# Neighbours' sums of six of ten node tiles by gathered rows instead of an adjacency product, in a graph network of two attention layers and a relational layer

## The chip, the cores and the metric

The kernel runs on one core of one Trainium2 chip. The metric is device time in microseconds (us) of one execution; the time before is the median of three runs. Five engines work side by side, each with an instruction queue of its own that runs in order: PE (TensorE, matrix products and transposes), DVE (VectorE), ACT (ScalarE), POOL (GpSimd, here mostly the issuer of indirect DMAs, which gather or scatter rows by an index), and SP (SyncE, issues plain DMAs). PEld is PE's weight load. DMA engines, 16 of them, move data for all queues.

## The reference, cut to what matters

1250 nodes of 768 features, 20000 edges (src, dst), each with one of 34 types.

```
x = x + GATv2(relu(layernorm(x)))          # two attention layers, 8 heads and 1 head
h = relu(layernorm(x))
mean[r, n] = mean over edges of type r into n of h[src]
h1  = sum over r of mean[r] @ W_rel[r] + h @ W_root + b_rgcn
xw  = h1 @ W_gcn
deg = (number of edges into a node) + 1;  dinv = rsqrt(deg)
out[n] = sum over edges into n of xw[src] * dinv[src] * dinv[n] + xw[n] * dinv[n]^2 + b_gcn
x + out
```

Everything is float32. The last layer is linear, so the kernel sums the scaled rows of h1 over the neighbours first and multiplies by W_gcn afterwards.

## The kernel before, in words

**Nodes by degree.** The front part sorts the nodes by falling degree into NT = 10 tiles of P = 128 (NP = 1280 places). Tile k has room for `CAPS[k]` edges per node: (33, 22, 20, 18, 17, 16, 15, 14, 13, 11), 179 slots in all. `f.srci[p, k, s]` is the source node of slot s of the node at place p of tile k, `f.pad` marks empty slots, `f.perm` the node of a place (`f.permg` the same, kept below 1250), `f.degf` the degree by place, `f.degn` the degree by node.

**Two attention stages.** For each slot a row of 768 features (and a few more numbers) per node is gathered on POOL into one of 24 buffers (`fs`, L1179 by the helper at L1125), DVE works out the logits (L1189 to L1195) and PE adds up the weighted rows. Between them POOL scatters one small record per slot (`f.rec`: source and own node) to its place in a list in DRAM (`pair_d`), which groups edges by type (`list_edges`, L1362). `finish2`, once per tile at the end of the second stage, writes x1 with the last bias, scatters h (`h2_d`) and the root term h @ W_root + b_rgcn into `h1_d` (L1451 to L1454).

**The relation stage.** For each type r there are PT = 4 tiles of pairs (and PX = 3 spare tiles); `lists` holds the pair list. `first_half` gathers h rows (`g`, with further rows added on DVE, L1549 to L1555) and transposes them; `second_half` multiplies by W_rel[r], copies PSUM to `y` on ACT (for the first two tiles scaled by `rcnt`, one over the number of edges of the pair, L1572; else L1574) and scatters `y` into `h1_d` with an adding DMA (L1575). Beside it, DVE builds a row of the adjacency matrix per place, one instruction per slot (`adjacency`, L1489, float16, 1250 columns), and when a tile's slots are done PE transposes the rows and ACT writes them into `adj`, scaled by dinv of the source (`adjacency_columns`, L1495 and L1497).

**The tail.** Once the last sum is in `h1_d`, it is loaded as ten tiles `h3` of 125 partitions (L1603, on SP's and ACT's queues in turn), `neighbours` multiplies them with `adj` for 512, 512 and 256 places (L1626; results to `gT` by ACT and DVE, L1629 and L1630), and `last(k)` multiplies one tile of places by W_gcn (L1638), scales by dinv of the place and adds x1 on DVE (L1641), and scatters to the output on POOL.

**What sets the order.** The code states the order of dependences only; a planner puts each engine's instructions in the order in which it expects them to become ready, and among ready ones in the order of the code. A tile with `bufs=n` is a ring of n buffers: the next user waits until the buffer's readers are done. `issue_after` holds an instruction behind a given one on its engine.

Of the kernel before, what the change touches and what calls it, by code (L numbers as in the profile page):

```python
# [27 lines left out]
PT = 4  # L28
PX = 3
# [596 lines left out]
def fast_front(ctx, tc, f, x, src, dst, edge_type, W1s, b1s, W1d, b1d, attn1, W_rel):  # L626
# [43 lines left out]
    f.srci = keepp.tile([P, NT, S0], I32, name="srci")  # L670
# [386 lines left out]
def halves(t, n, f):  # L1057
    return t[:n, :f.D].rearrange("p (a b) -> p a b", a=2)
# [45 lines left out]
def fast_rest(ctx, tc, f, x, src, dst, edge_type, W1s, b1s, W1d, b1d, attn1, ln1_w, ln1_b,  # L1104
# [10 lines left out]
    h1_d = dram.tile([NP + (PT + 1) * P, D], F32, name="r_h1_d")  # L1115
    pair_d = dram.tile([P * f.COLS, 2], I32, name="r_pair_d")
# [32 lines left out]
    def attention(H, table, negated, attn, first, loads, finish, rate, rest):  # L1149
# [25 lines left out]
        def front(c, i):  # L1175

            t, s = c.t, c.first + i
            fs = pool.tile([P, RW], F32, name="fs", tag="fs", bufs=ring)
            row = gather(fs[:, :W], table[:, :], f.srci[:, t.k, s:s + 1])  # L1179
            fs = fs[:, :W].rearrange("p (h e) -> p h e", h=H)  # L1180
            if s >= CHUNK or t.k:
                list_edges(row, rate)
            if t.k == NT - 1 and s == t.S - 1:
                list_edges(row, rest)
            if t.lg is None:
                lg = pool.tile([P, S0 * f.H], F32, name="lg", tag="lg", bufs=2)
# [143 lines left out]
    def prepare_lists():  # L1330
# [3 lines left out]
        with tc.tile_pool(name="r_fill", bufs=1, side="right") as fp:  # L1334
# [3 lines left out]
            fill = fp.tile([P, COLS, 2], I32, name="fill")  # L1338
# [16 lines left out]
        f.rec = rp.tile([P, NT, S0, 2], I32, name="rec")  # L1355
        nc.vector.tensor_copy(f.rec[:, :, :, 0], f.srci)
# [67 lines left out]
    with ExitStack() as two:  # L1424
        ap2 = two.enter_context(tc.tile_pool(name="r_att2", bufs=1, side="right"))

        def loads2():
            for name, a in (("lnw", lno_w), ("lnb", lno_b), ("bias_r", b_rgcn), ("bias_g", b_gcn)):
                late[name] = load_row(ap2, a, name)
            late["wroot"] = load_w(ap2, W_root, "wroot", "wroot")  # L1430

        def finish2(k, o):
            lnw, lnb, bias_r, bias_g = late["lnw"], late["lnb"], late["bias_r"], late["bias_g"]
# [31 lines left out]
    dinv = rq.tile([P, NT], F32, name="dinv")  # L1465
    nc.scalar.activation(dinv, f.degf, AF.Sqrt, bias=f.ones_col, scale=1.0)
    nc.vector.reciprocal(dinv, dinv)
    dinvn = rq.tile([P, NT], F32, name="dinvn")
    nc.scalar.activation(dinvn[:NQ], f.degn[:NQ], AF.Sqrt, bias=f.ones_col[:NQ], scale=1.0)
    nc.vector.reciprocal(dinvn[:NQ], dinvn[:NQ])  # L1470
# [9 lines left out]
    adj = rq.tile([P, NT, NP], F32, name="adj")  # L1480
# [10 lines left out]
    def adjacency_columns(k):  # L1491
# [4 lines left out]
        for j in range(NT):  # L1496
            nc.scalar.activation(adj[:NQ, j, k * P:(k + 1) * P], pt[:NQ, j, :], AF.Copy, scale=dinvn[:NQ, j:j + 1])  # L1497

    slots_left = [(k, s) for k in range(NT) for s in range(CAPS[k])]


    with ExitStack() as three:
# [3 lines left out]
        lists = gp.tile([P, COLS, 2], I32, name="lists")  # L1506
# [13 lines left out]
        nc.vector.reciprocal(rcnt, rcnt)  # L1520

# [5 lines left out]
        def first_half(i):  # L1527
# [13 lines left out]
            j.node = lists[:, col, 1:2]  # L1541
# [25 lines left out]
        def second_half(j, w):  # L1567
# [29 lines left out]
    with ExitStack() as four:  # L1597
# [17 lines left out]
        def neighbours(lo, hi):  # L1615

            if lo == 0:
                pss = [sums_psum() for _ in range(KC // 2)]
                order = [(j, c) for j in range(NT) for c in range(KC)]
            else:  # L1620
                pss = [None] * (KC // 2)
                order = [(j, 2 * g + c) for g in range(KC // 2) for j in range(NT) for c in range(2)]
            for j, c in order:
                if pss[c // 2] is None:
                    pss[c // 2] = sums_psum()
# [5 lines left out]

        def last(k):
            xt = gp.tile([P, D], F32, name="x1r", tag="x1r", bufs=3)
# [7 lines left out]
            nc.vector.scalar_tensor_tensor(halves(o, P, f), ps[:, :, :HW], dinv[:, k:k + 1], halves(xt, P, f),  # L1641
# [56 lines left out]
```

## Time and profile before

| what | value |
|---|---|
| median of three runs (lowest, highest) | 2852.77 us (2851.39, 2857.41) |
| profiled execution, and its span from the first to the last instruction | 2850.16 us, 2848.3 us |
| mean granted TensorE clock | 0.924 |
| PE, DVE, ACT, POOL busy | 84%, 57%, 30%, 52% of the span |
| first attention stage's gathers begin | 177 us |
| second attention stage's gathers begin | 941.5 us |
| relation stage's gathers begin | 1425.0 us |
| last `y` is scattered | 2615.1 us |
| first and last matmul of the tail | 2628.7 us, end 2837.3 us |

Times in the profile are from one execution and counted from its first instruction; a difference between two kernels' medians is compared with the sum made on it. A group line of the profile has line, engine, operation, out<-in, number of instructions, then busy time, mean duration of one in ns, and the engine's idle time just before them with what ended it. A line of a helper (L1125 gather, L1129 scatter, L1094 dense product, L1082 transposes) serves several stages, which the tile names tell apart. In a timeline line the numbers are start, duration, engine, line, and in brackets the engine's idle time before it and what ended it.

### The profile page before, as it was taken

To read this page: it belongs to the slowest core of one execution; us is meant where nothing else is said; L and a number is where in the kernel's file an instruction comes from. 1 tells how busy PE (TensorE), PEld (TensorE's weight loads), DVE (VectorE), ACT (ScalarE), POOL (GpSimd) and SP (SyncE) were. 2 spreads that over 40 slices of the span, in tenths; PEclk is the share of its full clock that TensorE was granted. 3 is DMA by queue.
4 is the path that set the end of the run, shared out by engine and by line. 5 is a ranking of instruction groups with operands and counts; after the bars stand their busy time and mean duration, and the time that the engine had idled before them with its cause. 6 is when DMAs were issued, how large, how long until landed. Compare 5 with 4: busy or idle time off the path is not lost. (4 is left out here: it accounts for less than half of the span.)

```text
span 2848.3 us, 24209 instructions
## 1 busy us (share of the span) xinstructions
PE 2391.8 (84%) x7859; PEld 1393.1 (49%) x7859; DVE 1621.7 (57%) x2382; ACT 846.5 (30%) x2320; POOL 1482.4 (52%) x1049
## 2 busy tenths in 40 slices
PE   5912574779998477888789999999999999997998
PEld 3411232445544244445456666666666666664455
DVE  5459988999986699999474433343343333210000
ACT  2000792778674022333211222222212212221000
POOL 2440787687786586777275555454455554421000
PEclk9955897999999688899889999999999999999999
DMA  5150643444540675676277777777777777665211
GB/s 199 28 188 31 199 137 94 124 133 119 146 146 28 224 233 181 200 222 204 100 228 201 188 187 196 195 201 180 181 201 182 183 198 185 182 163 130 82 45 50
DMA packets 130127, 448.22 MB, mean 157 GB/s; under 512 B 25014, under 2 KB 26061, under 8 KB 129991
## 3 DMA queue, kind: packets, MB, share of 16 engines
q0 software_dynamic: 77792, 305.26, 41.0%
q1 hardware_dynamic: 47257, 133.96, 13.3%
q10 hardware_dynamic: 4942, 7.36, 0.8%
q8 instruction: 65, 1.06, 0.1%
q14 instruction: 71, 0.58, 0.1%
HBM read 357.48 MB, written 89.11 MB: 157 GB/s over the span
## 5 line engine op out<-in xcount | busy, mean ns | idle before, releaser
L1094 PE MATMUL ps<-wrel,mT 128*128 128x384 f32 x3336 | 1099.5, 486 | 0.7 <-DMA wrel<-in_L_gnn_W_rel_dram 0.7
L1094 PEld LDWEIGHTS ps<-wrel,mT 128*128 128x128 f32 x3336 | 623.4, 190 | 406.8 <-DMA wrel<-in_L_gnn_W_rel_dram 1.0
L1125 POOL DMA_INDIRECT g<-r_h_d,lists x241 | 367.5, 1525 | 472.6 <-DVE g L1549 300.7
L1249 PE MATMUL ag<-fs,identf 128*128 128x384 f32 x716 | 285.6, 531 | 175.2 <-ACT fs L1247 163.1
L1247 ACT ACTIVATE fs<-fs,lg 128x96 f32<-128x96 f32 x1376 | 370.2, 362 | 1.7 <-issue 1.4
L1189 DVE TENSOR_TENSOR z<-fs,nfd 128x776 f32<-128x776 f32 (+1 forms) x358 | 344.5, 977 | 42.8 <-DMA fs<-f_fs_d,srci 25.2
L1549 DVE TENSOR_TENSOR g<-g,g 128x768 f32<-128x768 f32 x68 | 64.6, 950 | 525.8 <-DMA g<-r_h_d,lists 426.6
L1239 PE MATMUL ag<-fs,dg 128*128 128x384 f32 x716 | 251.6, 513 | 84.7 <-ACT dg L1237 84.7
L1129 POOL DMA_INDIRECT r_pair_d<-rec,place x179 | 242.3, 1354 | 126.7 <-DMA r_pair_d<-fill 72.4
L1575 POOL DMA_INDIRECT r_h_d<-y,lists x139 | 229.4, 1650 | 131.3 <-ACT y L1574 64.8
L1249 PEld LDWEIGHTS ag<-fs,identf 128*128 128x128 f32 x716 | 131.9, 200 | 316.3 <-ACT fs L1247 250.0
L1125 POOL DMA_INDIRECT fs<-f_fs_d,srci x179 | 238.5, 1332 | 90.9 <-issue 45.3
L1125 POOL DMA_INDIRECT fs<-r_fs_d,srci x179 | 240.2, 1342 | 84.9 <-PE ag L1239 38.3
L1489 DVE SCALAR_TENSOR_TENSOR arow<-node,from_f,arow 128x1250 f16<-128x1250 f16 x179 | 270.8, 1514 | 3.7
L1239 PEld LDWEIGHTS ag<-fs,dg 128*128 128x128 f32 x716 | 142.8, 202 | 188.4 <-ACT dg L1237 90.3
L1574 ACT COPY y<-ps 128x768 f32<-128x768 f32 x71 | 56.8, 800 | 481.3 <-PE ps L1094 481.3
L1572 ACT ACTIVATE y<-ps,rcnt 128x768 f32<-128x768 f32 x68 | 61.3, 901 | 444.8 <-PE ps L1094 444.8
L1191 DVE SCALAR_TENSOR_TENSOR z<-z,attn_e 128x769 f32<-128x769 f32 x179 | 178.5, 1017 | 0.0
L1194 DVE TENSOR_TENSOR z<-z,attn_e 128x776 f32<-128x776 f32 x179 | 168.4, 954 | 0.1
L1195 DVE TENSOR_REDUCE lg<-z 128x8 f32<-128x776 f32 x179 | 168.1, 950 | 0.1
L1630 DVE COPY gT<-hb 128x512 f32<-128x512 f32 (+1 forms) x9 | 5.4, 602 | 249.8 <-ACT gT L1629 249.8
L1626 PE MATMUL hb<-adj,h 125*128 125x512 f32 (+1 forms) x360 | 131.4, 528 | 14.7 <-DMA h<-r_h_d 14.7
(271 smaller groups left out, 2288.5 us busy)
## 6 DMA issues: line engine op xcount, KB each, us to landing
wrel<-in_L_gnn_W_rel_dram SPq DMA_DIRECT2D x37, 2304.0 KB
g<-r_h_d,lists POOLq DMA_INDIRECT x241
r_nfd_d<-fd SPq DMA_DIRECT2D x10, 384.0 KB
nfd<-r_nfd_d SPq DMA_DIRECT2D x10, 384.0 KB
r_x_d<-xb SPq DMA_DIRECT2D x10, 384.0 KB
x1r<-r_x_d SPq DMA_DIRECT2D x10, 384.0 KB
f_fs_d<-o_s SPq DMA_DIRECT2D x9, 388.0 KB
x<-in_x_dram SPq DMA_DIRECT2D x9, 384.0 KB
```

What stands on the lines that cost most here:

```text
L1094: last = nc.tensor.matmul(ps[:n, half, :f.HW], hT[:, k, j * P:j * P + n], w[:, k, cols], start=(k == 0), stop=(k == f.KC - 1 and not bias))
L1125: return nc.gpsimd.indirect_dma_start(out=to, out_offset=None, in_=table, in_offset=bass.IndirectOffsetOnAxis(ap=idx, axis=0))
L1129: s = nc.gpsimd.indirect_dma_start(out=table, out_offset=bass.IndirectOffsetOnAxis(ap=idx, axis=0), in_=rows, in_offset=None, **kw)
L1189: nc.vector.tensor_tensor(z, fs, t.nfd, op=ALU.max)
L1191: nc.vector.scalar_tensor_tensor(z[:, 0, :], z[:, 0, :], 1.0, attn_e[:, 0, :], op0=ALU.mult, op1=ALU.mult, accum_out=t.lg[:, s, :])
L1194: nc.vector.tensor_mul(z, z, attn_e)
L1195: nc.vector.tensor_reduce(t.lg[:, s, :], z, axis=AX.X, op=ALU.add)
L1239: nc.tensor.matmul(c.ps[:, half, :HW], dg, fs[:, 0, half * HW:(half + 1) * HW], start=begin, stop=end)
L1247: nc.scalar.activation(fs[:, h, :HD], fs[:, h, :HD], AF.Copy, scale=t.lg[:, s, h:h + 1])
L1249: nc.tensor.matmul(c.ps[:, half, :HW].rearrange("p (h d) -> p h d", d=HD), f.identf, fs[:, half * H // 2:(half + 1) * H // 2, :HD], start= ...
L1489: nc.vector.scalar_tensor_tensor(a, node16, from_f[:, k, s:s + 1], a, op0=ALU.is_equal, op1=ALU.add)
L1575: s = nc.gpsimd.indirect_dma_start(out=h1_d[:, :], out_offset=bass.IndirectOffsetOnAxis(ap=j.node, axis=0), in_=y, in_offset=None, compute ...
```

## The change: what it does

Four of the ten node tiles (k = 0 to 3, DT = 4, the highest degrees) keep the adjacency product: `adj` has 512 columns, `adjacency` and `adjacency_columns` run for 93 of 179 slots. For the other six, in the order 9 to 4, the new `by_rows(k)` gathers each node's own row of `h1_d` into an accumulator (`acc`, two buffers) and then one row per slot (`nb`, twelve buffers), which DVE adds; empty slots read a row of zeros at the end of `h1_d`. PE transposes the sum and ACT writes it to `gT`. `last(0)` to `last(3)` stand between them in the code, `last(9)` to `last(4)` behind them.

For the sum of rows to be right, the rows of `h1_d` must already be scaled by dinv of their node. So the pair records get a third number, dinv of the own node, from which every `y` is scaled on ACT (times one over the count for the first two tiles); the root term is scaled by dinv on ACT as it leaves PSUM, with its bias now added by PE as a product of a row of ones; and `adj` is no longer scaled. `f.srci` becomes the first column of `f.rec`.

```diff
-    f.srci = keepp.tile([P, NT, S0], I32, name="srci")
+    f.rec = keepp.tile([P, NT, S0, 3], I32, name="rec")
+    f.srci = f.rec[:, :, :, 0]
...
-            row = gather(fs[:, :W], table[:, :], f.srci[:, t.k, s:s + 1])
+            row = gather(fs[:, :W], table[:, :], f.rec[:, t.k, s, 0:1])
...
+            nc.sync.dma_start(h1_d[ZERO:, :], zero[:1])
...
-        nc.vector.tensor_copy(f.rec[:, :, :, 0], f.srci)
+        f.dinv = rp.tile([P, NT], F32, name="dinv")
+        nc.scalar.activation(f.dinv, f.degf, AF.Sqrt, bias=f.ones_col, scale=1.0)
+        nc.vector.reciprocal(f.dinv, f.dinv)
+        nc.vector.tensor_copy(f.rec[:, :, :, 2].bitcast(F32), f.dinv[:, :, None].to_broadcast([P, NT, S0]))
...
-            ps = dense(nc, ps_t, f, hT, late["wroot"], 0, P, tag="mm2")
+            ps, _ = dense(nc, ps_t, f, hT, late["wroot"], 0, P, tag="mm2", bias=(late["ones"], late["bias_r"]))
-            nc.vector.tensor_add(halves(o, P, f), ps[:, :, :HW], halves(bias_r, P, f))
+            nc.scalar.activation(halves(o, P, f), ps[:, :, :HW], AF.Copy, scale=f.dinv[:, k:k + 1])
...
-    adj = rq.tile([P, NT, NP], F32, name="adj")
+    adj = rq.tile([P, NT, DT * P], F32, name="adj")
+    srcz = rq.tile([P, NT, S0], I32, name="srcz")
+    nc.vector.scalar_tensor_tensor(srcz, f.pad, float(ZERO), f.srci, op0=ALU.mult, op1=ALU.max)
...
-            nc.scalar.activation(adj[:NQ, j, k * P:(k + 1) * P], pt[:NQ, j, :], AF.Copy, scale=dinvn[:NQ, j:j + 1])
-    slots_left = [(k, s) for k in range(NT) for s in range(CAPS[k])]
+            nc.scalar.copy(adj[:NQ, j, k * P:(k + 1) * P], pt[:NQ, j, :])
+    slots_left = [(k, s) for k in range(DT) for s in range(CAPS[k])]
...
+        norms = lists[:, :, 2].bitcast(F32)
+        nc.vector.tensor_mul(rcnt, rcnt, norms[:, :R * PC].rearrange("p (r c) -> p r c", c=PC)[:, :, :2])
...
-            if j.t < 2:
-                nc.scalar.activation(halves(y, P, f), ps[:, :, :HW], AF.Copy, scale=rcnt[:, j.r, j.t:j.t + 1])
-            else:
-                nc.scalar.copy(halves(y, P, f), ps[:, :, :HW])
+            nc.scalar.activation(halves(y, P, f), ps[:, :, :HW], AF.Copy, scale=j.scale)
...
+        def by_rows(k):
+            acc = gp.tile([P, D], F32, name="acc", tag="acc", bufs=2)
+            gather(acc, h1_d[:, :], f.permg[:, k:k + 1])
+            for i in range(CAPS[k]):
+                g = gp.tile([P, D], F32, name="nb", tag="nb", bufs=12)
+                gather(g, h1_d[:, :], srcz[:, k, i:i + 1])
+                nc.vector.tensor_add(acc, acc, g)
+            to_columns(nc, ps_t, f, gT, k, acc, P, both=True)
...
-            xt = gp.tile([P, D], F32, name="x1r", tag="x1r", bufs=3)
+            xt = gp.tile([P, D], F32, name="x1r", tag="x1r", bufs=2)
...
-        neighbours(0, 512)
-        neighbours(512, 1024)
-        for k in range(4):
-            last(k)
-        neighbours(1024, NP)
-        for k in range(4, NT):
-            last(k)
+        neighbours(0, DT * P)
+        for k in range(NT - 1, DT - 1, -1):
+            by_rows(k)
+            if NT - 1 - k < DT:
+                last(NT - 1 - k)
+        for k in range(NT - 1, DT - 1, -1):
+            last(k)
```

The row of the list that is filled ahead of the scatters (`fill`) also gets a third column, of zeros, and the list is 12 bytes per record where it was 8.

More of the change, by code (lines that the diff above doesn't have):

```diff
@@ L28 @@
 PT = 4
+DT = 4
 PX = 3
@@ L1114, in fast_rest @@
     h2_d = dram.tile([NP + P, D], F32, name="r_h2_d")
-    h1_d = dram.tile([NP + (PT + 1) * P, D], F32, name="r_h1_d")
-    pair_d = dram.tile([P * f.COLS, 2], I32, name="r_pair_d")
+    ZERO = NP + (PT + 1) * P
+    h1_d = dram.tile([ZERO + 1, D], F32, name="r_h1_d")
+    pair_d = dram.tile([P * f.COLS, 3], I32, name="r_pair_d")
     x1_d = dram.tile([NP, D], F32, name="r_x1_d")
@@ L1337, in prepare_lists @@
                            allow_small_or_imprecise_dtypes=True)
-            fill = fp.tile([P, COLS, 2], I32, name="fill")
+            fill = fp.tile([P, COLS, 3], I32, name="fill")
+            nc.vector.memset(fill[:, :, 2], 0)
             ones_c = fp.tile([P, COLS], F32, name="ones_c")
@@ L1352, in prepare_lists @@
                 nc.sync.dma_start(h1_d[NP + t * P:NP + (t + 1) * P, :], zero)
+            nc.sync.dma_start(h1_d[ZERO:, :], zero[:1])
         f.place = rp.tile([P, NT, S0], I32, name="place")
         nc.sync.dma_start(f.place, f.place_d.rearrange("p (k s) -> p k s", k=NT))
-        f.rec = rp.tile([P, NT, S0, 2], I32, name="rec")
-        nc.vector.tensor_copy(f.rec[:, :, :, 0], f.srci)
+        f.dinv = rp.tile([P, NT], F32, name="dinv")
+        nc.scalar.activation(f.dinv, f.degf, AF.Sqrt, bias=f.ones_col, scale=1.0)
+        nc.vector.reciprocal(f.dinv, f.dinv)
+        nc.vector.tensor_copy(f.rec[:, :, :, 2].bitcast(F32), f.dinv[:, :, None].to_broadcast([P, NT, S0]))
         nc.vector.tensor_copy(f.rec[:, :, :, 1], f.perm[:, :, None].to_broadcast([P, NT, S0]))
@@ L1427, in loads2 @@
         def loads2():
-            for name, a in (("lnw", lno_w), ("lnb", lno_b), ("bias_r", b_rgcn), ("bias_g", b_gcn)):
+            for name, a in (("lnw", lno_w), ("lnb", lno_b), ("bias_g", b_gcn)):
                 late[name] = load_row(ap2, a, name)
+            late["ones"] = ap2.tile([1, P], F32, name="ones_r")
+            nc.vector.memset(late["ones"], 1.0)
+            late["bias_r"] = ap2.tile([1, D], F32, name="bias_r")
+            nc.scalar.dma_start(late["bias_r"], bass.AP(tensor=b_rgcn.tensor, offset=b_rgcn.offset, ap=[[0, 1], [1, D]]))
             late["wroot"] = load_w(ap2, W_root, "wroot", "wroot")
         def finish2(k, o):
-            lnw, lnb, bias_r, bias_g = late["lnw"], late["lnb"], late["bias_r"], late["bias_g"]
+            lnw, lnb, bias_g = late["lnw"], late["lnb"], late["bias_g"]
             sc, sh = norm_scale(nc, small, f, o, P)
@@ L1464, in fast_rest @@
     rq = ctx.enter_context(tc.tile_pool(name="r_late", bufs=1))
[L1465 to L1470, printed above, removed]
     ident16 = rq.tile([P, P], F16, name="ident16")
@@ L1505, in fast_rest @@
         assert not edges
-        lists = gp.tile([P, COLS, 2], I32, name="lists")
+        lists = gp.tile([P, COLS, 3], I32, name="lists")
         nc.sync.dma_start(lists, pair_d.rearrange("(p c) f -> p c f", p=P))
@@ L1540, in first_half @@
                 col = r * PC + t
-            j.node = lists[:, col, 1:2]
+            j.node, j.scale = lists[:, col, 1:2], norms[:, col:col + 1]
+            if t < 2:
+                j.scale = rcnt[:, r, t:t + 1]
             g = gp.tile([P, D], F32, name="g", tag="g", bufs=7)
@@ L1615, in neighbours @@
         def neighbours(lo, hi):
[L1617 to L1625, printed above, removed]
+            pss = [sums_psum() for _ in range(KC // 2)]
+            for j, c in [(j, c) for j in range(NT) for c in range(KC)]:
                 nc.tensor.matmul(pss[c // 2][:, c % 2, :hi - lo], hs[j][:, c * P:(c + 1) * P], adj[:NQ, j, lo:hi],
@@ L1640, in last @@
             o = gp.tile([P, D], F32, name="o4", tag="o4", bufs=3)
-            nc.vector.scalar_tensor_tensor(halves(o, P, f), ps[:, :, :HW], dinv[:, k:k + 1], halves(xt, P, f),
+            nc.vector.scalar_tensor_tensor(halves(o, P, f), ps[:, :, :HW], f.dinv[:, k:k + 1], halves(xt, P, f),
                                            op0=ALU.mult, op1=ALU.add)
             scatter(out[:, :], o, f.perm[:, k:k + 1], "out", bounds_check=N - 1, oob_is_err=False)
-        neighbours(0, 512)
-        neighbours(512, 1024)
-        for k in range(4):
-            last(k)
-        neighbours(1024, NP)
-        for k in range(4, NT):
+        neighbours(0, DT * P)
[4 more added lines that the diff above has]
+        for k in range(NT - 1, DT - 1, -1):
             last(k)
```

## The prediction

> **What bounds the kernel now.** I read the page's slices first, for which engine is full where.
>
> ```profile
> PE   5912574779998477888789999999999999997998
> DVE  5459988999986699999474433343343333210000
> POOL 2440787687786586777275555454455554421000
> ```
>
> A slice is 71 us. DVE fills the attention slices (5 to 19), PE everything after slice 21. In the last three DVE is at 0 and POOL at 1, then 0: the tail is TensorE alone. The chain of waits, in order of time, says the same to the hundredth:
>
> ```profile
> 2615.09 5.49 DMA r_h_d<-y,lists
> ...
> 2628.65 105.36 PE hb L1626 x240
> 2734.01 30.96 PE hb L1638 x96
> 2764.97 25.90 PE hb L1626 x120
> 2790.88 46.46 PE hb L1638 x144
> ```
>
> The last h1 sum lands at 2620.6; the h rows are loaded; then PE runs without a gap to 2837.3: 131.3 us of adjacency product (L1626) and 77.4 of W_gcn product (L1638), the latter 7.74 per node tile. From PE's last matmul to the end of the span are 11.0 us. Next, busy time by window, for attention 2, the relation stage and the h loads (columns: window, its length, PE, PEld, DVE, ACT, POOL busy, clock, DMA share, GB/s):
>
> ```profile
> 1000.00:1370.00 370.00, 295.59 (x864) 170.92 (x863) 362.47 (x697) 111.93 (x235) 264.57 (x188) 0.89 0.65 201
> 1440.00:2614.00 1174.00, 1173.24 (x4261) 723.49 (x4260) 423.36 (x353) 247.76 (x514) 583.46 (x369) 1.00 0.72 186
> 2622.00:2634.00 12.00, 5.35 (x8) 2.38 (x9) 0.00 (x0) 0.00 (x0) 0.00 (x0) 0.54 0.32 124
> ```
>
> DVE binds attention 2 (98% busy), PE the relations (99.9%). While the h rows load, the DMA share is only 0.32 at 124 GB/s, so about a third of the DMA engines carry them.
>
> **The sum is made on the profiled execution**, 2850.16 us (span 2848.3 and 1.9 around it); the median of the three runs, 2852.77, lies 2.6 above it, and I add that at the end.
>
> **Part 1, attention 2: -7 us.** Ten PSUM evacuations of `root` leave DVE (L1453, 952 ns each, about 0.88 net since neighbouring instructions overlap by 0.07) for ACT, 30% busy in this window. Eight fall where DVE is full: 8 x 0.88 = 7.0. PE gets four bias instructions per tile (1.3 us at the 0.33 us pace of the dense ones) and has 74 idle us here. ACT now waits for the product where DVE did (L1453 waited 16.4 us in all), and ACT's diagonal scalings for PE queue behind it; the ring of 24 gathered rows covers a wait of a few us, without it this costs up to those 16. At the stage's end DVE no longer holds `x1` for a root, -2.6; the bias matmuls, ACT's turn and a pair list half as long again to load give back about 2. I count -0.5, between -2.5 and +2.
>
> **Part 2, relations: -4 us.** Six of ten tiles' transposes go (L1495, 7.4 us for ten: 4.4, or 3.5 by the 0.58 after which PE's next began). 86 adjacency instructions of 1.51 us leave DVE, which is 36% busy here: nothing. y is scaled on ACT always, 0.90 against 0.80 us, once on the path: +0.1.
>
> **Part 3, front: +0.5 us.** One memset of 241 columns (0.25), a reciprocal (0.14), and a copy for a copy of the same 330 elements on a full DVE. The square root and reciprocal move there from 1413. SP issues one more small write, some 0.5 us ahead of weights not needed for many us. Pair scatters carry 12 bytes for 8 in the same 128 rows: nothing. The gathers now read the tile whose other columns DVE fills. In the trace the copy of `perm` into it runs at 115.5, far ahead of its place in the code, and the first gather at 177; so I see no wait.
>
> **Part 4, the tail.** PE's work falls from 208.7 to 52.7 (half of 105.36) + 77.4 + 6 x 0.82 of transposes = 135 us. But 86 neighbour rows and 6 own rows have to be gathered, 92 POOL instructions, and added, 86 x 0.95 = 82 us on an idle DVE. What does a gather cost beside such adds? Nearest is the opening of attention 2: rows of the same 3 KB, a DVE that is 77% busy with instructions of two SBUF inputs (28.1 of the 36.5 us from 941.5), other loads beside it.
>
> ```profile
> 941.51 0.99 POOL L1125 DMA_INDIRECT fs<-r_fs_d,srci  x1 [2.99 <-DMA r_fs_d<-fs,f_perm]
> ...
> 976.92 1.29 POOL L1125 DMA_INDIRECT fs<-r_fs_d,srci  x1 [0.47 <-DMA wroot<-in_L_gnn_W_root_dram]
> ```
>
> 23 steps in 35.41 us: 1.54 each, and the row is usable 3.1 us after its issue ends (the first VectorE instruction on it starts at 945.62). Bounds: 1.25, the even step from 177 to 207, most of it with DVE idle; and 2.32, the mean step of the seven from 1438.64 to 1454.90, beside back-to-back 1.5 us instructions of L1489. I take 1.54. So POOL is the new bound: 92 x 1.54 + 10 x 1.3 of output scatters = 155 us.
>
> It cannot run through, for the change adds a wait. There are two accumulators: tile 7's own row waits until tile 9's transposes have read the first, and on PE these stand behind the whole product of tiles 0 to 3. Behind that gather POOL's queue holds tiles 6 to 4 and all outputs, and DVE's the adds of tile 7, which alone free the ring of twelve. Up to then POOL can do 12 + 14 gathers for tiles 9 and 8 and 12 into the ring for tile 7: 38. They collide with the h rows. How queues share busy engines is shown where all three were full (share of 16 engines):
>
> ```profile
> q0 software_dynamic: 301, 1.50, 47.2%
> q1 hardware_dynamic: 303, 0.93, 29.1%
> q10 hardware_dynamic: 301, 0.83, 26.3%
> ```
>
> Gathers (q0) take 47 of 102, so the h rows keep 54% of their 130 GB/s, 70: 3.84 MB need 55 us and the last lands near 2677; at 130 it would be 2651. PE has two slices of 5.14 left then, so the product ends near 2687, not 2682.5. A gather needs a third of its 393 KB from those same engines: 123 KB at 61 GB/s, 2.0 us each until 2677, 1.54 after: 34 landed by 2687.
>
> Then: 2687 + 1 (tile 9's transposes) + 58 x 1.54 = 89.3 + four outputs between, 5.2, gives 2782.5. On the path behind the last gather: landing 3.1, add 0.95, transposes 1.5 and W_gcn product 7.74 + 4 (the granted clock was 0.54 in the first 4 us after PE's last idle stretch, and PE will have idled), two copies 1.0: 18.3, so 2800.8, and 11.0 to the end: **2811.8, -36.5 against 2848.3**. The products of the other tiles fit into PE's pauses.
>
> [...]
>
> **Sum:** 2850.16 - 36.5 - 7 - 0.5 - 4 + 0.1 + 0.5 = 2802.8; with 2.6 for the median, **2805**.
>
> **The rivals.**
> *Cheap gathers* (10%): 1.25 and an uncontended load. T9 at 2683.5, 54 left: 67.5 + 5.2 + 18.3 + 11 = 2785.5 for the tail, 2779 in all. For it: the 1.25 rows; against: DVE will be busy.
> *The planned order stalls at the product's end* (12%): if POOL's order has the first output, or DVE's the copies of the product, before tile 8's rows are added, only 25 gathers precede 2688. At 1.64 each (1342 ns is the mean of attention 2's gathers, and 0.30 between them) 67 of them, 5.2 and 29.3 end the tail at 2832, -16; with gains of only 5 before it 2832 in all. For it: POOL and DVE are in order; against: in the relation stage's opening the first scatter of y came at 1456.07 behind 18 gathers, six us after y was ready, so the order leans to gathers.
> *Dear gathers, the slower side* (7%): at 2.32, 28 are done by 2687 and 64 remain: 2688 + 148.5 + 5.2 + 29.3 = 2871, +22.7, or 2864 in all. It decides from 2.2 us per gather (30 done, 62 x 2.2 = 136). For it: the rows at 1438; against: no 1.5 us VectorE instructions run in the tail.
> *Queues in code order* (5%): each output then waits for its tile's product and all later gathers behind it: 2695 after tile 9, then 14, 15, 16 gathers at 1.54 each with 16.8 for landing, add, transposes, product and output (2815), 35 gathers (2869), 7 and six products in a row (2922), 11: 2933, or 2926 in all. Against it stand the 18 gathers, where the code has five.
> *No net change* (2%): gathers near 2.2, PE's saving spent by POOL to the microsecond.
>
> **How the numbers follow.** The forecast has 64%; its own range is 2787 to 2822 (gathers at 1.35 to 1.75, product's end 2682 to 2690). The cheap and the stalled case take it to 2776 to 2834, which leaves out the two slow cases and a little beyond each end. A difference of 0.2%, 5.7 us, is about what measurement tells from none. Faster 0.64 + 0.10 + 0.12, less 0.01 for a tail worse than its bounds: 0.85; same 0.03, the last rival and that 0.01; slower 0.07 + 0.05 = 0.12.
>
> **What would show it.** Gathers `nb` at a mean step of 1.5 to 1.6; POOL the chain's main engine from 2677 to the last gather; a pause of POOL before tile 7's `acc`; h rows landing over some 55 us; L1626 at 120 instructions with gaps; attention 2 ending 7 us earlier. Wrong if the step exceeds 2.2, or if POOL sits before an `out` scatter for more than 10 us.

## The result, and the profile after

The changed kernel takes 2831.33 us (median of seven runs, 2824.57 to 2843.05) against 2852.77 before: ratio 0.9926, 95% interval 0.9904 to 0.9947. That is 21 us less, not 48. The profiled execution took 2831.33 as well; its span is 2829.2. Cut at the same five events in both traces:

| stretch (us) | before | changed | difference | predicted |
|---|---|---|---|---|
| start to the first gather of attention 2 | 941.5 | 941.6 | +0.1 | +0.5 |
| to the last weighted sum of attention 2 | 444.8 | 448.6 | +3.8 | -7 |
| to the first relation product | 54.1 | 54.2 | +0.1 | -0.5 |
| to the last relation product | 1173.6 | 1170.7 | -2.9 | -3.9 |
| to the end of the span | 234.3 | 214.0 | -20.3 | -36.5 |

So the front and the relations went as forecast, attention 2 went the other way, and the tail gained a little over half. The page's slices, the three rows that were shown of before:

```profile
PE   5912574788898377888969999999999999999676
DVE  5459988999987699899552223222222222200254
POOL 2440687687777576688264554445444454431465
```

In the last three slices PE is no longer full and DVE and POOL are no longer empty: the work did move. The question is what it waits for there. The windows of the tail (window, length, PE, PEld, DVE, ACT, POOL busy, clock, DMA share, GB/s):

```profile
2622.00:2634.00 12.00, 0.00 (x0) 0.00 (x0) 0.00 (x0) 0.00 (x0) 8.61 (x9) 0.50 0.81 240
2634.00:2690.00 56.00, 48.87 (x104) 20.70 (x105) 21.08 (x22) 0.00 (x0) 26.76 (x23) 0.93 0.83 260
2690.00:2722.00 32.00, 27.14 (x82) 15.12 (x81) 13.45 (x15) 3.38 (x7) 15.84 (x14) 0.95 0.66 215
2722.00:2790.00 68.00, 48.16 (x144) 28.16 (x143) 41.03 (x44) 1.82 (x4) 53.21 (x49) 0.87 0.91 312
```

POOL issues 23 gathers in the 56 us of the second line, one in 2.4 us, and 49 gathers and scatters in the 68 us of the last. The DMA share is not full in the slow stretch, 0.83. PE's groups in order of time, and POOL at the end of that stretch (start, duration; in brackets the idle time before and what ended it), say why:

```profile
2634.92 22.85 PE L1627 MATMUL hb<-adj,h 125*128 125x512 f32 x48 [19.70 <-DMA nb<-r_h_d,srcz]
2661.22 12.27 PE L1627 MATMUL hb<-adj,h 125*128 125x512 f32 x24 [3.46 <-DMA h<-r_h_d]
2673.99 10.57 PE L1627 MATMUL hb<-adj,h 125*128 125x512 f32 x24 [0.50 <-DMA h<-r_h_d]
2686.81 10.57 PE L1627 MATMUL hb<-adj,h 125*128 125x512 f32 x24 [2.25 <-DMA h<-r_h_d]
```

```profile
2647.64 1.13 POOL L1128 DMA_INDIRECT nb<-r_h_d,srcz  x1 [1.08 <-DMA nb<-r_h_d,srcz]
2649.90 1.13 POOL L1128 DMA_INDIRECT nb<-r_h_d,srcz  x1 [1.14 <-DMA nb<-r_h_d,srcz]
...
2700.80 0.94 POOL L1128 DMA_INDIRECT acc<-r_h_d,f_permg  x1 [0.64 <-issue]
2712.16 1.54 POOL L1128 DMA_INDIRECT nb<-r_h_d,srcz  x1 [10.42 <-DVE acc L1640]
```

PE waits for h rows again and again; the last two come at 2686.8. POOL in turn waits for earlier gathered rows to land. Tile 7's own row goes out at 2700.8, behind 12 of its neighbour rows, takes 10.05 us to land, and POOL stands for 10.42 us with a full ring. One more stop stands near the end of the chain of waits, where the profile can name no releaser:

```profile
2779.55 0.96 issue
2780.55 12.69 another core or an unknown queue
2793.40 0.79 issue
2794.20 0.96 DVE acc L1640
```

### The profile page after: what moved, and what is told of

It is laid out like the page before. It is cut to its first block, busy times and chain, and to the rows that moved or that the text cites. A ratio compares the mean times of both kernels' runs of the same rounds, so it can differ in the third digit from the quotient of the medians.

```text
span 2829.2 us, 23953 instructions
## 1 busy us (share of the span) xinstructions
PE 2348.8 (83%) x7635; PEld 1358.1 (48%) x7635; DVE 1563.6 (55%) x2363; ACT 845.0 (30%) x2275; POOL 1554.3 (55%) x1141
## 5 line engine op out<-in xcount | busy, mean ns | idle before, releaser
L1128 POOL DMA_INDIRECT g<-r_h_d,lists x241 | 340.0, 1411 | 526.8 <-DVE g L1560 286.3
L1242 PE MATMUL ag<-fs,dg 128*128 128x384 f32 x716 | 250.0, 511 | 81.0 <-ACT dg L1240 42.2
L1128 POOL DMA_INDIRECT fs<-f_fs_d,rec x179 | 237.6, 1327 | 90.0 <-issue 48.4
L1583 POOL DMA_INDIRECT r_h_d<-y,lists x139 | 223.0, 1604 | 108.7 <-ACT y L1582 51.3
L1128 POOL DMA_INDIRECT fs<-r_fs_d,rec x179 | 237.5, 1327 | 81.5 <-issue 34.3
L1582 ACT ACTIVATE y<-ps,lists 128x768 f32<-128x768 f32 x71 | 64.0, 901 | 479.1 <-PE ps L1096 479.1
L1582 ACT ACTIVATE y<-ps,rcnt 128x768 f32<-128x768 f32 x68 | 61.3, 902 | 457.4 <-PE ps L1096 443.9
L1640 DVE TENSOR_TENSOR acc<-acc,nb 128x768 f32<-128x768 f32 x86 | 81.5, 957 | 192.6 <-DMA h<-r_h_d 129.2
L1496 DVE SCALAR_TENSOR_TENSOR arow<-node,from_f,arow 128x1250 f16<-128x1250 f16 x93 | 140.3, 1508 | 1.0
L1128 POOL DMA_INDIRECT nb<-r_h_d,srcz x86 | 95.7, 1113 | 65.1 <-DMA nb<-r_h_d,srcz 27.8
```

Source lines behind the costliest of these rows:

```text
L1128: return nc.gpsimd.indirect_dma_start(out=to, out_offset=None, in_=table, in_offset=bass.IndirectOffsetOnAxis(ap=idx, axis=0))
L1242: nc.tensor.matmul(c.ps[:, half, :HW], dg, fs[:, 0, half * HW:(half + 1) * HW], start=begin, stop=end)
L1496: nc.vector.scalar_tensor_tensor(a, node16, from_f[:, k, s:s + 1], a, op0=ALU.is_equal, op1=ALU.add)
L1583: s = nc.gpsimd.indirect_dma_start(out=h1_d[:, :], out_offset=bass.IndirectOffsetOnAxis(ap=j.node, axis=0), in_=y, in_offset=None, compute ...
```

## The experiments

Each kernel was compared with the kernel before on the same chip (before: 2825.58 us for the first four, 2849.46, 2848.79, 2826.24 and 2851.89 for the later groups), so only ratios are compared between groups. "Att 2" is the second line of the table above, "tail" the time from the start of the h loads to the end of the span, "last row" the issue of the last neighbour row in that tail. The figures for attention 2 in the expectations are 1.1 to 1.7 us too long throughout, because the last gather was counted twice; the table has them right. The last three columns come from one profile each, or from two where two figures stand.

| kernel | ratio (95%) | att 2 | tail | last row |
|---|---|---|---|---|
| before (profiles 1, 2) | 1 | 444.8, 443.7 | 227.4, 227.5 | |
| changed (profiles 1, 2) | 0.992 (0.9906 to 0.9935) | 448.6, 446.8 | 207.2, 203.6 | 175.2, 175.2 |
| upstream | 1.0021 (1.0010 to 1.0032) | 453.0 | 226.9 | |
| rows128 | 0.9824 (0.9808 to 0.9840) | 448.3 | 176.6 | 149.2 |
| oneload | one profile | 447.1 | 179.7 | 151.7 |
| rootvec | 0.9926 (0.9897 to 0.9955) | 445.7 | 202.1 | 175.0 |
| nobias | one profile | 442.5 | 201.9 | 173.9 |
| rows128acc | 0.9874 (0.9849 to 0.9898) | 448.9 | 189.1 | 147.1 |
| pre | 0.9831 (0.9818 to 0.9844) | 447.4 | 178.3 | 149.6 |
| prebias | 0.9850 (0.9811 to 0.9888) | 441.6 | 175.5 | 147.5 |
| prebias5 | 0.9844 (0.9831 to 0.9858) | 443.9 | 182.3 | 137.9 |
| all | 0.9846 (0.9833 to 0.9860) | 443.8 | 185.0 | 142.6 |
| copies | 0.9860 (0.9840 to 0.9880) | 447.3 | 187.1 | 144.8 |
| planned | 0.9813 (0.9794 to 0.9833) | 441.7 | 173.8 | 148.1 |
| product128 | 1.0014 (0.9991 to 1.0038) | 447.7 | 224.0 | |

**The changed kernel again.** No edit.

> The changed kernel once more, for a second profile of it. Theory A: the 13 us in which PE's columns stopped between 2780 and 2793, with the sixth tile's evacuation and 14 queued adds behind it, belong to the way the tail is ordered and come again in a second profile, within 3 us of the same place. Rival: they are an accident of one execution; then the last neighbour row is issued some 8 us earlier and the span is 5 to 9 us shorter than 2829. Either way the ratio to the kernel before is 0.990 to 0.995.

Ratio 0.992. The stop did not come again; PE's groups in the same stretch of the second profile:

```profile
2748.62 18.87 PE L1649 MATMUL hb<-wgcn,gT 128*128 128x384 f32 x58
2775.50 1.51 PE L1084 MATMUL pt<-identf,acc 128*128 128x128 f32 x6 [8.01 <-DVE acc L1640]
```

58 instructions without a break, where the first profile has 17 and then single ones. The tail is 3.6 us shorter, less than the rival's 5 to 9, because the last row is issued at the same 175.2 us in both. So the stop is an accident of one execution, worth 3.6 us by these two profiles; the change gains 20 us in the tail with it and 24 without.

**Everything ahead of the tail alone.**

```diff
-    adj = rq.tile([P, NT, DT * P], F32, name="adj")
+    adj = rq.tile([P, NT, NP], F32, name="adj")
...
-        neighbours(0, DT * P)
-        for k in range(NT - 1, DT - 1, -1):
-            by_rows(k)
...
+        neighbours(0, 512)
+        neighbours(512, 1024)
+        for k in range(4):
+            last(k)
+        neighbours(1024, NP)
+        for k in range(4, NT):
+            last(k)
```

> All ten tiles go by the adjacency product again, as before the change; everything ahead of the tail stays changed (third number in the pair records, root scaled on ACT, bias by PE, unscaled adjacency). My prediction gave this part -11 us less the transposes that return (4.4 at most): a median of 2846 or less, ratio 0.9975 or less. Theory B, from the two traces (attention 2 ends 1.7 later, the relation stage starts 4.1 later and is 2.9 shorter for its missing transposes): +4 us, ratio 1.000 to 1.003, and then the whole gain of the change lies in the tail.

1.0021, 2.8 to 9.0 us slower than before: Theory B's range. My -11 for the parts ahead of the tail is refuted: without the saved transposes they cost time, and the gain lies in the tail.

**The h rows over all DMA engines.**

```diff
-    nc.gpsimd.iota(node16, pattern=[[1, NT], [NT, NQ]], base=0, channel_multiplier=0,
+    nc.gpsimd.iota(node16, pattern=[[P, NT], [1, P]], base=0, channel_multiplier=0,
...
-        h1n = h1_d[:N, :].rearrange("(p j) d -> p j d", j=NT)
...
-            h = gp.tile([NQ, D], F32, name="h3", tag="h3", bufs=NT)
-            (nc.sync, nc.scalar)[j % 2].dma_start(h, h1n[:, j, :])
+            h = gp.tile([P, D], F32, name="h3", tag="h3", bufs=NT)
+            (nc.sync, nc.scalar)[j % 2].dma_start(h, h1_d[j * P:(j + 1) * P, :])
```

> The h rows are loaded as ten tiles of 128 rows (node = 128 j + p) in place of 125 rows; the adjacency rows get 1280 columns to match. Theory C: the tail lost its time in the first 70 us because the 125-row loads were carried by a third of the DMA engines, which the gathers load as well; over all engines the rows land by 2650, the product ends at 2688 to 2692 (2697 with the change), gathers step at 1.4 to 1.7 us while it runs (2.5 with the change), tile 9 and 8 and the ring are full by 2680, and the last gather is issued near 2775: 12 to 25 us less than the changed kernel, ratio to the kernel before 0.984 to 0.989. Rival D: the steps of 2.5 us are the price of a gather beside adds, whatever else is loaded; then the product gains at most 6 us and the end at most 8, ratio 0.990 to 0.993.

Ratio 0.9824, better than either theory said: 27 us off the tail of the second profile. The product now runs from 4.0 to 58.3 us of the tail without a break, and the DMA engines are full while the rows come (windows 0 to 8, 8 to 40 and 40 to 59 us of the tail):

```profile
2599.81 54.30 PE L1626 MATMUL hb<-adj,h 128*128 128x512 f32 x120 [10.40 <-DMA h<-r_h_d]
```

```profile
2595.80:2603.80 8.00, 3.99 (x5) 1.85 (x6) 0.00 (x0) 0.00 (x0) 5.79 (x6) 0.50 0.89 312
2603.80:2635.80 32.00, 32.00 (x74) 14.02 (x73) 15.34 (x16) 0.00 (x0) 22.98 (x20) 0.98 1.02 400
2635.80:2654.80 19.00, 19.00 (x50) 8.78 (x49) 9.08 (x11) 1.83 (x4) 14.47 (x13) 1.00 0.92 323
```

400 GB/s where the changed kernel moved 260. Rival D falls. Theory C has one gap left: a load now also takes 128 adjoining rows where it took every tenth row. The last run of this section closes it.

**One h load in place of ten.**

```diff
-            h = gp.tile([NQ, D], F32, name="h3", tag="h3", bufs=NT)
-            (nc.sync, nc.scalar)[j % 2].dma_start(h, h1n[:, j, :])
+            if j == 0:
+                h = gp.tile([NQ, D], F32, name="h3", tag="h3", bufs=NT)
+            if j:
+                h = hs[0]
+            else:
+                nc.sync.dma_start(h, h1n[:, j, :])
```

> Leaves out nine of the ten h loads: the product takes all its rows from the first one. Theory C: with no rows beside them the gathers of the first 70 us step at 1.25 to 1.5 us, 38 are issued by 2675, the product runs without a wait from 2628 and ends near 2688; POOL then waits 10 us or more for the accumulator. Rival D: the gathers still step at 2.3 us or more, and POOL has no wait for the accumulator.

With nine loads gone the first 37 steps of POOL take 1.46 us on average. They are 1.25 where the adds leave gaps, and near 2 beside adds that run without a break:

```profile
2618.80 0.95 POOL L1128 DMA_INDIRECT nb<-r_h_d,srcz  x1 [0.30 <-DVE acc L1644]
2620.05 0.95 POOL L1128 DMA_INDIRECT nb<-r_h_d,srcz  x1 [0.30 <-DVE acc L1644]
2621.31 1.04 POOL L1128 DMA_INDIRECT nb<-r_h_d,srcz  x1 [0.30 <-issue]
...
2624.62 1.68 POOL L1128 DMA_INDIRECT nb<-r_h_d,srcz  x1 [0.31 <-DVE acc L1644]
2626.61 1.68 POOL L1128 DMA_INDIRECT nb<-r_h_d,srcz  x1 [0.30 <-DVE acc L1644]
```

```profile
2622.53 7.91 DVE L1644 TENSOR_TENSOR acc<-acc,nb 128x768 f32<-128x768 f32 x8 [1.00 <-DMA nb<-r_h_d,srcz]
```

The issue of a gather grows with what is left of the add that runs when it begins. Of the 92 gathers here, the 49 that begin with no add running take 0.95 us (median); the 24 that begin with 0.6 us or more of an add to go take 1.65.

POOL stops for tile 7's accumulator from 55.4 to 62.0 us, 6.6 where Theory C had 10 or more, and for the row in it until 67.3. A gather beside adds takes 1.25 to 2 us a step, then; what the changed kernel's 2.4 have beyond that was the h rows' doing. The tail, 179.7 us, is no shorter than with all ten loads spread (176.6): spread, they cost nothing that shows.

**The kernel before again.** No edit.

> The kernel before once more, for a second profile of it beside the others of this chip. Attention 2 (first to last gather) at 399.7 us in its first profile: 398 to 402 expected; from there to the relation stage's first gather 83.8: 82 to 86; the stage to its last product 1189: the same within 1.

This execution was long (2893.0 us), but the extra lies in attention 1: attention 2's first gather comes at 985.2. Behind it all is as in the first profile: 443.7, 53.2, 1174.7 and 234.4 against 444.8, 54.1, 1173.6 and 234.3. Differences of 2 us in the stretches ahead of the tail mean little. This kernel's tail repeats to 0.1 us; the changed one's does not (207.2, 203.6).

**The root term back on DVE.**

```diff
-            ps, _ = dense(nc, ps_t, f, hT, late["wroot"], 0, P, tag="mm2", bias=(late["ones"], late["bias_r"]))
+            ps = dense(nc, ps_t, f, hT, late["wroot"], 0, P, tag="mm2")
-            nc.scalar.activation(halves(o, P, f), ps[:, :, :HW], AF.Copy, scale=f.dinv[:, k:k + 1])
+            nc.vector.scalar_tensor_tensor(halves(o, P, f), ps[:, :, :HW], f.dinv[:, k:k + 1],
+                                           halves(late["bias_r"], P, f), op0=ALU.mult, op1=ALU.add)
```

> On the changed kernel the root term alone goes back: DVE evacuates it again (scaled by dinv and bias added in one instruction), the bias product of PE goes. Leaves out the scaling of the bias, which is zero in these data. Theory E: attention 2 is a closed loop (gathered rows, logits on DVE, diagonals on ACT, sums on PE, which free the rows), so what left DVE came back on PE and ACT: first to last gather 399 to 402 us, no different from the change (401.3, 401.7), and the stretch from there to the relation stage 82 to 85. My prediction's view: DVE binds attention 2, and 8 x 0.88 on it again make it 407 to 409.

**No bias product on PE.** Only the first two lines of that diff.

> The changed kernel without the bias product on PE (leaves the root bias out; it is zero in these data); ACT still evacuates and scales. Theory E1: the four bias instructions, 1 us a tile in PE's order ahead of the sums, are what took the gain back: first to last gather 392 to 396 us. Theory E2: it is ACT, where the diagonals stand behind a root evacuation that waited 7.7 us for its product: 400 to 402 us. The relation stage and the tail as in the changed kernel within 4 us.

(These two texts take the root bias for zero, and it is not: rootvec's and nobias's sums differ in value by what they leave out. The instructions that remain are the same.) Attention 2 takes 445.7 us with the root on DVE and 442.5 without the bias product, against 448.6 and 446.8. My view needed 407 to 409 from the start of the first gather to the end of the last; it was 400.9, inside Theory E's 399 to 402. So ten evacuations on DVE are worth nothing like 7 us: nobias, which has them on ACT, is 1.2 and 2.3 us below the two profiles of before, and prebias and planned, which follow and have a root instruction on DVE again, take 441.6 and 441.7. The bias products are what cost: with them eight profiles have 446.8 to 448.9 and a ninth (upstream) 453.0, without them eight have 441.6 to 445.7, before included. The medians are 447.7 and 443.8. The groups of PE and ACT in the changed kernel, from 1000 to 1345 us:

```profile
L1100 PE MATMUL ps<-bias_r,ones_r 1*128 1x384 f32 x28 | 12.7, 533 | 0.0
```

```profile
L1464 ACT ACTIVATE root<-ps,dinv 128x768 f32<-128x768 f32 x7 | 6.3, 896 | 53.9 <-PE ps L1100 53.9
```

They stand in PE's order ahead of weighted sums, and the sums free the ring of rows; that they cost time in this way was not shown. DVE's z in the same window of the changed kernel shows where its free time went:

```profile
L1192 DVE TENSOR_TENSOR z<-fs,nfd 128x769 f32<-128x769 f32 x143 | 146.0, 1044 | 9.8 <-DMA fs<-r_fs_d,rec 9.6
```

In the kernel before it had 4.1 us of idle time ahead of it, here 9.8, and its mean grew from 1010 to 1044 ns. By the measure that the expectations named, first to last gather, nobias has 402.0 us and E2 seems to hold; the difference sits behind the last gather, from whose start to the last weighted sum it takes 42.2 us in place of 46.8 to 48.3 in the changed kernel. So E1 named the right part, at some 4 us and not 7, and in the wrong place. E was right in that DVE alone does not set the pace.

**Six accumulators.** On rows128:

```diff
-            acc = gp.tile([P, D], F32, name="acc", tag="acc", bufs=2)
+            acc = (gp.tile([P, D], F32, name="acc", tag="acc", bufs=2) if k >= NT - 2 else
+                   work.tile([P, D], F32, name="acc", tag=("att_o", "att_e")[k % 2]))
```

> The 128-row loads, and six accumulators in place of two (four of them in buffers left from the attention stages), so that no own row waits for an earlier tile's transposes. Theory F: with two, POOL stopped from the 59th to the 65th us of the tail and all later tiles were late by as much; without that stop the last row is issued near 135 us after the h loads begin (149 with the loads alone), PE's queue of W_gcn products becomes the end, and the tail takes 160 to 170 us (176.6): ratio to the kernel before 0.976 to 0.981. Rival G: from there on the gathers are bound by what the DMA engines carry (1.25 us for 393 KB) and the stop is caught up: less than 4 us, ratio 0.981 to 0.983.

Slower than rows128, 0.9874, and outside the ranges of both theories. POOL no longer stops for an accumulator, but the last row is issued at 147.1 us, not 135, and PE stands for 14 us behind the product and tile 9's transposes:

```profile
2677.86 0.82 PE L1084 MATMUL pt<-identf,acc 128*128 128x128 f32 x6
2692.95 7.39 PE L1649 MATMUL hb<-wgcn,gT 128*128 128x384 f32 x17 [14.27 <-DVE gT L1630]
```

I read this as W_gcn landing late and built the next runs on it. The line says something else: DVE's `gT`.

**W_gcn loaded early; then the bias on DVE; then five tiles by the product.** On rows128:

```diff
+            nc.sync.dma_start(f.w1d, W_gcn.rearrange("(k p) n -> p k n", p=P))
...
-        wgcn = load_w(gp, W_gcn, "wgcn")
+        wgcn = f.w1d
```

> The 128-row loads with two accumulators, and W_gcn loaded in attention 2 into the buffer of a weight that is no longer needed, so that its 2.36 MB leave the tail. Theory H: with the rows spread the tail is bound by what all DMA engines carry, some 50 MB in 150 us; 2.36 MB fewer make it 7 us shorter: last neighbour row near 142 us after the h loads begin (149 with the 128-row loads alone), tail from there to the end 168 to 172 (176.6), ratio to the kernel before 0.979 to 0.981. Rival: the waits for accumulators and the order of the output scatters bind it; then within 2 us of 176.6, ratio 0.982 to 0.983.

2.36 MB fewer in the tail changed nothing (178.3 us, last row at 149.6). Theory H falls; the rival's numbers came, its cause is taken up below.

```diff
-            ps, _ = dense(nc, ps_t, f, hT, late["wroot"], 0, P, tag="mm2", bias=(late["ones"], late["bias_r"]))
+            ps = dense(nc, ps_t, f, hT, late["wroot"], 0, P, tag="mm2")
...
-            nc.scalar.activation(halves(o, P, f), ps[:, :, :HW], AF.Copy, scale=f.dinv[:, k:k + 1])
+            nc.vector.tensor_add(halves(o, P, f), ps[:, :, :HW], halves(late["bias_r"], P, f))
+            nc.scalar.activation(o, o, AF.Copy, scale=f.dinv[:, k:k + 1])
```

> As the run before it, and the root's bias is added on DVE, as before the change, and then scaled on ACT in place; PE's bias products go. From the first gather of attention 2 to its last weighted sum the kernel before took 446.0 and 444.9 us, the changed one 448.0 to 450.5 in five profiles, without the bias products 444.2. Theory I: PE's bias products, ahead of the sums in its order, cost these 4 us, and DVE's instruction costs 1 or 2: 445 to 447 here, ratio 0.001 below that of the run before it. Rival: the four us belong to ACT's part; then 448 to 450.

Attention 2 took 441.6 us, 5.8 below pre: the way of Theory I, and more than it had. By the medians (2801.54 against 2801.94) nothing of that reached the end; the interval is too wide to say more. From the weighted sums to the first relation product the profile shows 56.0 where pre has 52.2.

```diff
-DT = 4
+DT = 5
-        neighbours(0, DT * P)
+        neighbours(0, 512)
+        neighbours(512, DT * P)
```

> As the run before it, with five tiles by the product instead of four (DT = 5, a second pass of 128 places): 18 gathers fewer, 7.1 MB or 22 us at 320 GB/s, for 120 short products, 14 to 19 us, and the transposes of one more tile ahead of the tail. Theory H: gathers end near 122 us after the h loads begin; PE has 4 + 54 + 17 + 79 + 8 = 162 us without a pause and becomes the bound: end at 168 to 176, ratio within 0.002 of the run before it. Rival: the waits between the engines are what is long, and fewer gathers shorten each: 158 to 165.

Fewer gathers end earlier (137.9 us), but not near 122, because POOL now stops for the accumulator from 57.6 to 72.2 us, until the longer product is done. PE waits twice more, 7.3 and 4.9 us, for accumulators and ends at 173.8. The tail is 182.3 us against 175.5, the ratio 0.9844 against 0.9850: five tiles are no better, and the medians do not tell the two apart.

**All four steps together.**

> Four steps together on the changed kernel: 128-row loads, W_gcn loaded in attention 2, six accumulators, the root's bias on DVE. Theory J: with 128-row loads the tail is bound by POOL's stops (53 to 65 us for the accumulator, and the output scatters that wait for products); the six accumulators did nothing alone because PE then stood without W_gcn from 58 to 72 us and DVE's first output, waiting for that, held the adds behind it. With W_gcn there, POOL has no stop over 4 us before 70 us, the last row is issued at 120 to 135 us (148.7), and PE's 68 instructions behind the last transposes (23 us) and 10 to the end make the tail 158 to 170 us: ratio 0.975 to 0.980. Rival: the output scatters hold POOL as before and the last row stays at 145 to 149; with 23 us of products behind it the tail is 185 to 190, ratio 0.985 to 0.988.

0.9846: no better than rows128 alone. With W_gcn in place PE stood just as long, so its landing was not the cause:

```profile
2655.14 0.82 PE L1084 MATMUL pt<-identf,acc 128*128 128x128 f32 x6
2669.77 2.92 PE L1647 MATMUL hb<-f_w1d,gT 128*128 128x384 f32 x4 [13.80 <-DVE gT L1628]
```

```profile
2668.15 0.96 DVE L1638 TENSOR_TENSOR acc<-acc,nb 128x768 f32<-128x768 f32 x1 [0.39 <-DMA nb<-r_h_d,srcz]
2669.03 0.68 DVE L1628 COPY gT<-hb 128x512 f32<-128x512 f32 x1
2669.71 0.96 DVE L1638 TENSOR_TENSOR acc<-acc,nb 128x768 f32<-128x768 f32 x1
2670.59 0.68 DVE L1628 COPY gT<-hb 128x512 f32<-128x512 f32 x1
```

DVE's three copies of the product's sums, which every first W_gcn product needs, are planned behind 40 to 42 adds, and each add waits for its row. With two accumulators they stand behind 24. Theory J falls, and so does its reading of rows128acc.

**The copies on ACT, and PE's order written out.** On pre with six accumulators; the second also with the bias as in prebias:

```diff
-                    nc.vector.tensor_copy(gT[:, c, lo:hi], pss[c // 2][:, 1, :hi - lo])
+                    nc.scalar.copy(gT[:, c, lo:hi], pss[c // 2][:, 1, :hi - lo])
```

> 128-row loads, W_gcn loaded early, six accumulators, and the six copies of the product's sums to gT all on ACT (three were on DVE). Theory K: with six accumulators PE stood from 57 to 72 us because DVE's three copies were planned behind 40 to 42 adds, and those wait for rows; W_gcn's landing, which I had blamed, had nothing to do with it. With the copies on ACT PE goes on at 59 us, the outputs are ready 13 us earlier, the gathers end at 128 to 140 us (144 and 149 before) and the tail is 165 to 177 us, 23 of them products behind the last transposes. Rival: the rows land no faster than the gathers went; the last row stays at 144 to 149 and the tail at 183 to 190.

```diff
...
+        then = {9: (0,), 8: (1, 9), 7: (2, 8), 6: (3, 7), 5: (6, 5), 4: (4,)}
...
+            with tc.issue_after(mm.ins) if mm else ExitStack():
+                to_columns(nc, ps_t, f, gT, k, acc, P, both=True)
+            for i in then[k]:
+                mm = last(i)
```

> As the run before it, with the order of PE in the tail written out: the transposes of each tile are held behind the W_gcn products of the tiles that are ready earlier, so that one product and not three stands behind the last transposes; and the root's bias on DVE. Theory K: 15 us of products leave the end, the tail is 150 to 163 us, attention 2 (first gather to last weighted sum) 443 to 446, ratio to the kernel before 0.973 to 0.979. Rival: the rows land no faster; last row at 144 to 149, tail 170 to 176, ratio 0.981 to 0.984.

PE goes on at 58.7 us, as Theory K said. The first output does not come 13 us earlier, though: it is at 88.0 in copies (84.6 in all), behind 50 adds on DVE. The last row stays at 144.8 and 148.1, the rivals' 144 to 149. Writing out PE's order gives what it could, one product behind the last transposes instead of three: tail 173.8 against 187.1 (planned also has the bias on DVE), ratio 0.9813. That is not distinguishable from rows128 alone (0.9824). In both kernels PE also issued slowly for 17 and 25 us from the 70th on, for a reason that the profile does not name (told at the end), so that the price of PE's order alone is not settled.

**All tiles by the product, rows in 128-row tiles.** The edits of upstream and rows128 together.

> All ten tiles by the product as in the kernel before, the parts ahead of the tail as changed, and the rows loaded as 128-row tiles. Theory C: loads over a third of the engines cost the kernel before little, since nothing ran beside them; first product 4 us after the loads begin in place of 7.7, and from the last relation product to the end 229 to 232 us (234.3 and 234.4 in the kernel before). Then the change to gathered rows is worth near 50 us where the loads are spread (183) and 24 where they are not. Rival: the loads are as dear without gathers; then 215 to 222, and the change itself is worth only 35.

From the last relation product to the end: 230.7 us, against 233.5 in upstream and 234.3 before; the first product 3.7 us after the loads begin. The window from 2 to 10 us behind their start:

```profile
2631.00:2639.00 8.00, 6.18 (x8) 2.71 (x9) 0.00 (x0) 0.00 (x0) 0.00 (x0) 0.52 1.02 406
```

406 GB/s at a share of 1.02, where the kernel before moved 124 at 0.32: 25 and 24 GB/s for each busy engine. So it is the number of engines that the new shape changes, and not what one engine carries from adjoining rows. Theory C holds. Spreading the loads is worth 3 us to a kernel whose tail has nothing beside them, and 27 to the changed one. With spread loads gathered rows take 183.0 us there (rows128) instead of 230.7, 48 us less.

## Why the prediction was right and wrong

**Right:** the bound before (PE alone in the tail), the direction, the relations (-2.9 for -3.9), the front, a pause of POOL at tile 7's own row (behind it, though, not before it), and that output scatters would not ruin POOL's order. The price of 1.54 us for a gather was right as an average: with the loads spread POOL takes 1.57 a step, outputs included. The slow rivals did not come about; that the result, 2831, stands beside the stalled order's 2832 is chance, for 30 gathers and not 25 preceded 2688. The prediction's own sign of being wrong, a step above 2.2, did come, 2.4 us from 2634 to 2690, but through waits for landing rows.

The price of a single gather depends on the add beside it, though, and there one figure for all was too simple. In oneload a gather's issue takes 0.95 us with no add running (median of 49) and 1.65 with 0.6 us or more of an add still to run (median of 24), and its step beside adds without a break is near 2, not far from the 2.2 above which the prediction called itself wrong. The average is lower because 49 of the 92 gathers begin with no add running: the adds wait for their rows and leave gaps. What in an add holds an issue up was not shown.

**Attention 2, -7 predicted, +3.8 found.** The step that failed is "Eight fall where DVE is full: 8 x 0.88 = 7.0". A DVE that is 98% busy was taken for the bound. As I read it now, it is one station of a closed loop of gathered rows, logits, softmax, diagonals and sums with 24 buffers. Taking 7 us from one station gave nothing clear of the profiles' scatter (nobias is 1.2 and 2.3 us below before); adding the bias products to another, counted at nothing because PE had 74 idle us, cost some 4. They also took 0.45 us each, 12.7 for 28, where the prediction had 0.33.

**The tail, -36.5 predicted, -20.3 in the first profile and -24 in the second.** The mechanism was right, the h rows and the gathers on the same third of the engines; the step that failed is the size of its term, "the h rows keep 54% of their 130 GB/s, 70". I gave the rows 70 GB/s and the last at 2677; it came at 2686.8, 3.84 MB in 64.8 us, 59 GB/s, and the product ended at 2697.4 instead of 2687. The gathers beside it took 2.4 us, not 2.0. Tile 7's own row then went out at 2700.8, 12.8 us later than the sum had it. Ring and queue were full by then, so the remaining 54 gathers and outputs took 96.4 us where I had 94.5 for 58, with 10.42 us of it standing for one landing, 10.05 from the start of its issue, which I had put at 4.1. Behind the last row came 32.0 us (29.3 in the sum), 3.6 of them the accident. 12.8 + 1.9 + 2.7 = 17.4; less 1.2, by which the whole tail began later, these are the 16.2 that are missing.

What I had not seen is that the collision could be removed. 125 rows go to a third of the engines: that share, 0.32 in the window I printed, was read as a property of loads and not as a fault of their shape. With loads alone on the queues the share is 0.32 for 125 rows (before) and 1.02 for 128 rows (product128). Why the one shape goes to a third of the engines and the other to all of them was not shown.

**The accumulator wait,** the other half of my argument, is real (POOL stopped 5 to 11 us at it in every kernel with two accumulators and four tiles, 19 with five) but not what sets the end once the rows are spread: in all seven kernels with spread loads and four tiles, four of them without it, the last row came between 142.6 and 149.6 us. What sets it is POOL, the bound that the prediction named. Its groups in rows128, from the first gather to the last row:

```profile
L1128 POOL DMA_INDIRECT nb<-r_h_d,srcz x86 | 100.3, 1166 | 33.7 <-issue 21.6 <-DVE acc L1639 9.3 <-DMA nb<-r_h_d,srcz 2.0
L1128 POOL DMA_INDIRECT acc<-r_h_d,f_permg x6 | 7.1, 1191 | 6.5 <-DMA r_h_d<-y,lists 4.2 <-issue 0.9 <-PE pt L1084 0.9
L1132 POOL DMA_INDIRECT out_dram<-o,f_perm x4 | 5.1, 1281 | 1.3 <-DVE o L1651 0.4 <-DMA nb<-r_h_d,srcz 0.3 <-DVE acc L1639 0.3
```

It is busy for 112.5 us, and the 0.30 us that stand between any two of its instructions make 29 more: 141 of the 148.7 us. All other waits are 8 us there, and 5 to 8 in each of the seven kernels, so nothing that only shortens a wait can bring much: not more accumulators, not 2.36 MB fewer, not copies moved to ACT. At 0.95 us each the 92 gathers would take 87 us in place of 107; the 20 between go, by the reading of oneload, to the adds beside them.

**The better version** is the change with 128-row loads: 0.9824 of the kernel before, 50 us. No further step beat it measurably.

## What to carry to other kernels

When a change puts new DMA traffic beside an old load, look at how many engines carry the old load: a shape that left two thirds of them idle cost little alone here (3 us) and much in company (27). An engine at 98% in a closed loop with a finite ring did not pay out here what was taken from it (1.2 and 2.3 us of 7, in nobias), and "idle" time of the engine that received the work was not free (some 4 us). When a wait is taken away and nothing moves, read which instruction the released engine waits for next, with its releaser in brackets, before blaming a transfer: here the bracket said DVE's copy from the start. And before a transfer or a wait is called the bound, add up the busy time and the fixed pauses of the engine that issues: here they were 141 of 149 us.

## What the hardware showed unexpectedly

In three of the profiled tails PE, waiting for nothing that the profile shows, issued its instructions singly, a weight load or a matmul every 0.70 or 1.40 us, for some 5 us in the first profile of the change, 17 in copies and 25 in planned:

```profile
2695.30 0.48 PE L1650 MATMUL hb<-f_w1d,gT 128*128 128x384 f32 x1 [0.49 <-issue]
2696.76 0.48 PE L1650 MATMUL hb<-f_w1d,gT 128*128 128x384 f32 x1 [0.97 <-issue]
...
2702.39 0.80 PE L1650 MATMUL hb<-f_w1d,gT 128*128 128x384 f32 x1 [1.99 <-issue]
```

The granted clock falls to 0.50 meanwhile (copies, 2699.0 to 2711.8), as in the pause before the first product (2622 to 2634). The same code ran without it in the second profile of the change. The profile names no releaser, and its cause was not looked for in a run.

Attention 1 took 44 us longer in one execution of the kernel before (985.2 for 941.5 us to the first gather of attention 2) while every later stretch kept its length to 1.1 us.
